# The inverse column transform of a Haar layer: VectorE butterflies in place of matmuls for the first 16 channels of three batches, and the levels of the other chunks placed anew

## The chip, the cores and the metric

The kernel runs on one core of one Trainium2 chip. The metric is the device time of one execution in microseconds (us); of several runs the median is given. The engines of the core work beside each other, each in the order of its own instructions: TensorE (PE, with its weight loads PEld), VectorE (DVE), ScalarE (ACT), GpSimd (POOL), and SyncE (SP), which here issues most of the DMAs.

## What is computed

The input x is (4, 64, 256, 256) in float32: 4 batches of 64 channels. Four layers follow each other. Layers 0, 1 and 3 are a long convolution per channel with a separable filter; layer 2 works on a Haar transform.

```python
# layers 0, 1, 3: the filter of a channel is an outer product of two 256-long filters
k = einsum('ijk,imk->ijmk', hx, hy)
y = irfft2(rfft2(x, s=(512, 512)) * rfft2(k, s=(512, 512)) / 512)[..., :256, :256]
x = y + x * bias[:, None, None]
# layer 2
f1 = haar2d(x)                       # along w, then along h
for i in range(2):
    f4 = einsum('bchw,oc->bohw', f1 * v[i], conv_w[i])     # mixes the 64 channels
    acc += sign(f4) * relu(abs(f4) - tau[i])
x = haar2d(acc, inverse=True) + x
```

One level of the inverse Haar transform takes sums and differences of two halves, a + d and a - d, and doubles the length; eight levels make 256.

## The kernel before, in words

**Convolutions** (`first`, `second`, `contract`, lines 250 to 287). A separable convolution is two products with a Toeplitz matrix, one along each axis. `toeplitz` loads a [128, 2, 256] tile `t` from a padded filter in DRAM by an overlapping access pattern; `contract` makes four float32 matmuls of it (128x256 and 128x128, twice, L253 and L254). The first product goes to PSUM and is copied by ACT (L267), the second is added to the residual by DVE (L284). Layers 0 and 1 give a0, y0, a1, y1 per channel; then `pairs` (L329, L330) takes sums and differences of neighbours, `levels` the further levels along w (DVE L342, L343, then POOL), `store` keeps the result in DRAM, `split`, `rest`, `down` (L361, L366, L373) transform along h by a matmul with the Haar matrix, and `away` (L385, L386) stores the coefficients in DRAM.

**Mixing** (`mixing`, lines 417 to 507). 64 groups per batch. A group loads two rows of coefficients of all channels (f), mixes the channels by 8 matmuls (L441, px), scales (L460 by DVE, L465 by ACT), takes size and sign on ACT (L469, L472), shrinks and signs on DVE (L476, L480), and adds the two terms into z (L486, DVE). z is one tile of SBUF, [128, 4, 128, 4, 16]: 4 chunks of 16 channels each, 128 places along h, 4 x 16 values per place.

**Inverse** (`inverse`, lines 509 to 597). The transform along h is made in one of two ways.
- By butterflies on DVE, in place in z: `level(n, chunk)` calls `halve`, which makes two DVE instructions (L291 a difference, L292 twice the even part less that difference), on 64 n elements each. The levels n = 1, 2, 4, ..., 64 are called for chunks 1, 2 and 3 (channels 16 to 63), n = 32 in two and n = 64 in four pieces of 16 pairs. `butterfly` makes the coarsest step for all chunks.
- For channels 0 to 15 (chunk 0), by a matmul per channel: `halves` splits the row-transformed tile pw into two parts w (ACT L540 and DVE L541), and `cols` multiplies both with the Haar matrix hb (two 128x512 matmuls, L547, pu).

Per channel: `sooner` loads the Toeplitz tile t2, `early` loads r, the untransformed part, from `keep` (tags f with three buffers or f4 with two; f4 holds also w), `fetch` copies the channel out of z (ACT L526, zc), `rows` makes the last steps along w and transposes (6 PE instructions, L533, L534, pw; the pool psx has two buffers), `join` adds r (DVE L555, t, one buffer) and takes sum and difference (L558, L559, u, five buffers). Then the last convolution follows (a3, y3, out), for two of three channels at once; of the third, `aside` stores u in DRAM (late), and its convolution is made during the mixing of the last batch.

**Order.** Work of different stages is interleaved by hand: each stage calls `at(time, run, unit)`, with a tick and a place in it from the table PLACE, and at the end all events run in the order of their times. A tick is one group of mixing or one channel of the inverse. The tile framework then orders each engine's instructions, may move one forward whose inputs are there, and puts in the waits; so the levels 16, 32 and 64 of batches 0 to 2, whose ticks lie in the inverse, stand for the most part in the mixing of the built program. Batch 0's convolutions stand alone at first; those of batch b + 1 are spread over the mixing of batch b, with a tail in the first channels of its inverse. The inverse of batch b runs from tick `start` to `start + 64`, then the mixing of batch b + 1 begins. `along` is the tick at which the batch's mixing starts. The last batch (b + 1 == B) has no convolutions to lay beside its mixing but those put aside, and its chunks' levels stand in its inverse.

Of the kernel before, what the change touches and what calls it, by code (L numbers as in the profile page):

```python
# [12 lines left out]
ALU = mybir.AluOpType  # L13
# [3 lines left out]
B, C, S, EMB, ORD = 4, 64, 256, 33, 64  # L17
# [8 lines left out]
PLACE = {  # L26
    "load": 0.714,
    "a0": 1.643,
    "a0 copy": 1.643,
    "y0": 2.571,  # L30
    "y0 sum": 2.571,
    "a1": 3.5,
    "a1 copy": 3.5,
    "y1": 4.429,
# [64 lines left out]
def conv_seq_kernel(ctx, tc, x, fz, fw, bias, decay, haar, haar_row, factors, vt, taut, wmix, out):  # L99
# [14 lines left out]
    nc = tc.nc  # L114
# [126 lines left out]
    def toeplitz(layer, c, name):  # L241

        t = tp.tile([P, 2, S], F32, name=name, tag="toep")
        nc.sync.dma_start(t, ap(pads[layer], c * 2 * ROW, [[1, P], [ROW, 2], [1, S]]))
        return t
# [40 lines left out]

        return [product, residual]

    def halve(even, odd):

        nc.vector.tensor_sub(odd, even, odd)  # L291
        nc.vector.scalar_tensor_tensor(even, even, 2.0, odd, ALU.mult, ALU.subtract)  # L292

    def level(n, chunk, begin=0, count=None):

        count = n if count is None else count
        v = z.rearrange("p n s x c -> p n s (x c)")[:, chunk].rearrange("p (j e s) x -> p j e s x", e=2, s=P // 2 // n)
        halve(v[:, begin : begin + count, 0, 0, :], v[:, begin : begin + count, 1, 0, :])

    def butterfly():  # L300

        v = z.rearrange("p n s (h k) c -> p n s h k c", k=2)
        for h in range(2):
            halve(v[:, :, 0, h, 0, :], v[:, :, 0, h, 1, :])
# [6 lines left out]
    def at(time, run, unit):  # L311
        events.append((time, len(events), run, unit))
# [196 lines left out]
    def inverse(b, start, put_off):  # L509

        st = {}

        def early(c):
            tag, bufs = ("f", 3) if c < 20 or c % 5 < 3 else ("f4", 2)
            r = mx.tile([P, 2, 2, P], F32, name=f"r_{b}_{c}", tag=tag, bufs=bufs)
            nc.sync.dma_start(r, keep[b][c])
            st[c]["r"] = r

        def sooner(c):
            st[c] = {}  # L520
            if c not in put_off:
                st[c][2] = toeplitz(2, c, f"t2_{b}_{c}")

        def fetch(c):
            a = mx.tile([P, 2, 2, P], F32, name=f"zc_{b}_{c}", tag="mag")
            nc.scalar.copy(a.rearrange("p h k i -> p (h k) i"), z[:, c // 16, :, :, c % 16].rearrange("p i x -> p x i"))  # L526
            st[c]["z"] = a

        def rows(c):
            a = st[c]["z"]  # L530
            ps = psx.tile([P, 2, 2, 2, P], F32, name=f"pw_{b}_{c}", tag="mix")[:, 0]
            for m in range(2):
                nc.tensor.matmul(ps[:, 0, m, :], a[:, 0, m, :], hsinv, start=True, stop=True)  # L533
                nc.tensor.transpose(ps[:, 1, m, :], a[:, 1, m, :], ident)  # L534
            st[c]["pw"] = ps

        def halves(c):
            w = st[c]["w"] = mx.tile([P, 2, 2, 2, P], F32R, name=f"w_{b}_{c}", tag="f4")
            ps = st[c]["pw"]
            nc.scalar.copy(w[:, 0], ps)  # L540
            nc.vector.tensor_tensor(w[:, 1], ps, w[:, 0].bitcast(F32), ALU.subtract)  # L541

        def cols(c):
            ps = psm.tile([P, 2, 2, P], F32, name=f"pu_{b}_{c}", tag="mm")
            flat = "p e m w -> p (e m w)"
            for i in range(2):
                nc.tensor.matmul(  # L547
                    ps.rearrange(flat), hb, st[c]["w"][:, i].rearrange(flat), start=(i == 0), stop=(i == 1)
                )
            st[c]["pw"] = ps  # L550

        def join(c):
            ps = st[c]["pw"]
            t = io.tile([P, 2, 2, P], F32, name=f"t_{b}_{c}", tag="res", bufs=BUFS["res"])
            nc.vector.scalar_tensor_tensor(t, st[c]["r"], 0.5, ps, ALU.mult, ALU.add)  # L555
            u = io.tile([P, 2, S], F32, name=f"u_{b}_{c}", tag="y", bufs=BUFS["y"])
            v = u.rearrange("p m (w e) -> p m w e", e=2)
            nc.vector.tensor_add(v[:, :, :, 0], t[:, 0], t[:, 1])  # L558
            nc.vector.tensor_sub(v[:, :, :, 1], t[:, 0], t[:, 1])  # L559
            st[c]["u"] = u  # L560

        def aside(c):
            nc.scalar.dma_start(late[b, c], st.pop(c)["u"])

        along = start - groups - 3

        def when(tick, n, chunk, *span):
            at(tick + PLACE["level"], lambda _: level(n, chunk, *span), 0)

        at(along + 11 + PLACE["level"], lambda _: butterfly(), 0)  # L570
        for chunk in range(1, 4):
            turn = start + 16 * (chunk - 1)
            for n in (1, 2, 4, 8):
                when(along + 12 + 3 * chunk if b + 1 < B else turn, n, chunk)
            when(turn + 1, 16, chunk)
            for i in range(2):
                when(turn + 2 + 2 * i, 32, chunk, 16 * i, 16)
            for i in range(4):
                when(turn + 6 + 2 * i, 64, chunk, 16 * i, 16)

        for c in range(C):
            for name, stage in zip(("sooner", "early", "fetch", "rows"), (sooner, early, fetch, rows)):
                at(start + c + PLACE[name], stage, c)
            turn = start + c
            if c < 16:
                at(start + c + PLACE["halves"], halves, c)
                at(start + c + PLACE["cols"], cols, c)
                turn += 1
            at(turn + PLACE["join"], join, c)
            if c in put_off:  # L590
                at(turn + PLACE["aside"], aside, c)
            else:
                shift = (0.0, 0.0)
                if put_off:
                    shift = ((-0.27, -0.342), (0.23, 0.158))[c % 3]
                for name, stage in zip(("a3", "a3 copy", "y3", "y3 sum", "out"), last(b, st)):
                    at(turn + PLACE[name] + shift[name[0] != "a"], stage, c)

    def last(b, st):
        return [  # L600
            *first(b, st, "u", 2, "a3"),
            *second(b, st, "a3", 2, "u", "y3", "co"),
            lambda c: nc.scalar.dma_start(out[b, c].rearrange("(k p) w -> p k w", p=P), st.pop(c)["y3"]),
        ]
# [40 lines left out]
    ahead = C  # L645
    start = ready + 3
    for b in range(B):
        mixing(b, start, N_ACT[b])
        end = start + groups + 3
        if b + 1 < B:  # L650
            ready = convolutions(b + 1, spread(ahead, end + 2), in_parts=range(C), border=end)
        else:
            convolution(
                [(i, c) for i in range(B - 1) for c in sorted(put_off)], spread(start - 2, end + 2, (B - 1) * len(put_off))
            )
        inverse(b, end, put_off if b + 1 < B else ())

        start = max(end + C, ready + 3)
        ahead = start - 3
# [114 lines left out]
```

## Time and profile before

| what | value |
|---|---|
| median of 3 runs | 2877.69 us (2876.81 to 2878.61) |
| the profiled execution | 2882.3 us, span of its instructions 2880.5 us |
| granted TensorE clock, mean | 0.998 |
| busy PE / PEld / DVE / ACT / POOL | 2825.3 / 2553.6 / 2504.8 / 2057.4 / 333.1 us |
| DMA | 649.77 MB, mean 226 GB/s |
| batch 0: first mixing matmul, first and last row matmuls | 450.7, 871.4, 1068.2 us |
| batch 1: the same | 1069.6, 1530.5, 1716.8 us |
| batch 2: the same | 1718.2, 2179.0, 2362.4 us |
| batch 3: the same | 2362.5, 2653.1, 2869.6 us |

In the lists of groups each line has the source line, the engine, the operation, out<-in by the names of the tiles, the shapes, the count, then the busy time and the mean time of one, and behind the second bar the idle time of the engine just before these instructions and what ended it. The busy time of an engine is the union of its instructions; an instruction may start before the one in front of it has ended, so a mean duration is more than what the instruction takes from a full engine. A window line gives busy time and count per engine between two times, then the granted clock, the share of the DMA engines and their rate.

### The profile page before, as it was taken

What the parts mean: (1) busy time and instruction counts of PE and PEld (TensorE: products, weight loads), DVE (VectorE), ACT (ScalarE), POOL (GpSimd) and SP (SyncE); (2) the same over time, 40 slices, a digit from 0 to 9 for tenths busy, and PEclk for the clock granted to TensorE, in tenths of its full rate; (3) what the DMA queues carried; (4) which work ended last, traced back from release to release, by engine and by line L of the source; (5) the groups of instructions that cost most, each with busy time, mean ns of one, the idle gap of its engine ahead of it and who ended that gap; (6) DMA issues with size and microseconds to landing.
All of it is one profiled execution on the core that took longest, in us unless ns stands there. A gap on an engine that the chain in (4) does not pass through costs nothing.

```text
span 2880.5 us, 52311 instructions
## 1 busy us (share of the span) xinstructions
PE 2825.3 (98%) x16566; PEld 2553.6 (89%) x16566; DVE 2504.8 (87%) x4263; ACT 2057.4 (71%) x4822; POOL 333.1 (12%) x644
## 2 busy tenths in 40 slices
PE   8999999999999999999999999999999999999999
PEld 6899998888888898998888998998888998888998
DVE  4655558999999779999999779999999779999985
ACT  2333337999995558989995658989995658888554
POOL 0111111121221001121121001121121000000000
PEclk9999999999999999999999999999999999999999
DMA  5877777676666986777777986777777988887786
GB/s 162 247 233 230 232 233 227 204 213 205 201 210 207 285 258 195 215 211 212 214 208 229 302 260 195 215 212 213 213 208 228 300 270 233 237 231 212 224 240 200
DMA packets 599366, 649.77 MB, mean 226 GB/s; under 512 B 48465, under 2 KB 517044, under 8 KB 598964
## 3 DMA queue, kind: packets, MB, share of 16 engines
q1 hardware_dynamic: 519860, 562.09, 67.1%
q10 hardware_dynamic: 79232, 84.34, 8.3%
q8 instruction: 134, 2.20, 0.3%
q14 instruction: 140, 1.15, 0.1%
HBM read 426.77 MB, written 219.48 MB: 224 GB/s over the span
## 4 chain that ended last, share of the span: by engine, by line
PE 47%; DVE 12%; ACT 3%; DMA 3%; issue 2%; POOL 0%; SPq 0%; DVEq 0%; ACTq 0%
PE pa L253 12%; PE py L253 11%; PE px L441 6%; PE pa L254 6%; PE py L254 6%; PE pw L533 4%; DVE mag L480 2%; DVE mag L476 2%; DVE y L284 2%; ACT f L465 2%; PE pw L534 2%; PE pz L373 2%; DVE f L460 1%; DMA t<-pad 1%; DVE z L486 1%
## 5 line engine op out<-in xcount | busy, mean ns | idle before, releaser
L253 PE MATMUL py<-t,a 128*128 128x256 f32 x3072 | 924.1, 383 | 10.1 <-ACT a L267 9.3
L267 ACT COPY a<-pa 128x512 f32<-128x512 f32 x768 | 478.6, 623 | 501.2 <-PE pa L254 462.9
L465 ACT ACTIVATE f<-px,vt 128x64 f32<-128x64 f32 x2688 | 584.7, 367 | 106.1 <-DVE f L460 105.8
L254 PEld LDWEIGHTS py<-t,a 128*128 128x128 f32 x3072 | 584.4, 190 | 79.6
L254 PE MATMUL py<-t,a 128*128 128x128 f32 x3072 | 590.8, 274 | 0.0
L253 PEld LDWEIGHTS py<-t,a 128*128 128x128 f32 x3072 | 497.5, 191 | 52.8 <-ACT a L267 20.1
L441 PE MATMUL px<-wb,f 128*128 128x256 f32 x2048 | 487.2, 380 | 6.3 <-ACT f L465 6.1
L441 PEld LDWEIGHTS px<-wb,f 128*128 128x128 f32 x2048 | 369.2, 190 | 48.0 <-ACT f L465 8.4
L343 POOL TENSOR_TENSOR sd<-less 128x128 f32<-128x128 f32 (+4 forms) x320 | 192.6, 602 | 1869.0 <-DVE less L342 1545.5
L526 ACT COPY zc<-z 128x512 f32<-128x512 f32 x256 | 281.7, 1103 | 107.8 <-PE pw L534 99.5
L476 DVE TENSOR_TENSOR mag<-mag,vt 128x1024 f32<-128x1024 f32 x256 | 312.2, 1220 | 11.5 <-ACT mag L469 10.7
L253 PE MATMUL pa<-t,y 128*128 128x256 f32 x1024 | 309.1, 384 | 7.9 <-DVE y L284 5.2
L480 DVE SCALAR_TENSOR_TENSOR mag<-mag,f 128x1024 f32<-128x1024 f32 x256 | 312.1, 1220 | 0.0
L469 ACT ACTIVATE mag<-f 128x1024 f32<-128x1024 f32 x256 | 295.4, 1154 | 22.9 <-DVE z L486 22.3
L253 PE MATMUL pa<-t,x 128*128 128x256 f32 x1024 | 306.2, 381 | 0.0
L366 DVE TENSOR_TENSOR sp<-sd,sp 128x512 fp32r<-128x512 f32 x256 | 178.7, 698 | 127.5 <-ACT sp L361 126.4
L472 ACT ACTIVATE f<-f 128x1024 f32<-128x1024 f32 x256 | 285.8, 1117 | 3.3
L253 PE MATMUL pa<-t,u 128*128 128x256 f32 x772 | 233.8, 385 | 6.5 <-ACT w L540 2.8
L284 DVE SCALAR_TENSOR_TENSOR y<-x,bsb,py 128x512 f32<-128x512 f32 x256 | 189.5, 740 | 44.6 <-PE py L254 43.6
L254 PEld LDWEIGHTS pa<-t,x 128*128 128x128 f32 x1024 | 194.8, 190 | 26.4
L254 PEld LDWEIGHTS pa<-t,y 128*128 128x128 f32 x1024 | 194.5, 190 | 26.3
L284 DVE SCALAR_TENSOR_TENSOR y<-y,bsb,py 128x512 f32<-128x512 f32 x256 | 189.3, 739 | 29.5 <-PE py L254 29.1
(72 smaller groups left out, 4393.2 us busy)
## 6 DMA issues: line engine op xcount, KB each, us to landing
t<-pad SPq DMA_DIRECT2D x768, 256.0 KB, 4.1
x<-in_x SPq DMA_DIRECT2D x256, 256.0 KB, 3.8
coef<-co SPq DMA_DIRECT2D x256, 256.0 KB, 3.2
f<-coef SPq DMA_DIRECT2D x256, 256.0 KB, 3.2
r<-keep SPq DMA_DIRECT2D x256, 256.0 KB, 4.2
out_y<-y ACTq DMA_DIRECT2D x256, 256.0 KB, 4.3
keep<-sums SPq DMA_DIRECT2D x256, 128.0 KB, 2.9
keep<-sd SPq DMA_DIRECT2D x256, 128.0 KB, 2.9
```

Source lines behind the costliest of these rows:

```text
L253: nc.tensor.matmul(ps[:, m, :], src[:, 0, m * P : (m + 1) * P], t[:, ::-1], start=True, stop=False)
L254: nc.tensor.matmul(ps[:, m, P:], src[:, 1, m * P : (m + 1) * P], t[:, : P - 1 : -1], start=False, stop=True)
L267: nc.scalar.copy(a, s["p" + new])
L284: nc.vector.scalar_tensor_tensor(y, s[res], bsb[:, layer, c : c + 1], s["p" + new], ALU.mult, ALU.add)
L343: engine.tensor_tensor(t[:, :, :, half:length], v[..., 0], v[..., 1], ALU.subtract)
L441: nc.tensor.matmul(ps[:, q, h, :], f[:, q, h * P : (h + 1) * P], wb.rearrange("p r n -> p (r n)"), start=True, stop=True,)
L465: nc.scalar.mul(f4[:, j], px[:, j], scale(g, 0)[:, j : j + 1])
L469: nc.scalar.activation(mag, st[g]["f4"], AF.Abs)
L472: nc.scalar.activation(st[g]["f4"], st[g]["f4"], AF.Sign)
L476: nc.vector.tensor_sub(mag, mag, over(g, 1, 16))
L480: nc.vector.scalar_tensor_tensor(mag, mag, 0.0, st[g]["f4"], ALU.max, ALU.mult)
L526: nc.scalar.copy(a.rearrange("p h k i -> p (h k) i"), z[:, c // 16, :, :, c % 16].rearrange("p i x -> p x i"))
```

## The change

In batches 0, 1 and 2 the matmul way of chunk 0 (`halves`, `cols`) is left out, and `level` is called for all four chunks. The levels n = 1 to 16 of every chunk stand in the mixing; n = 32 of chunks 0 and 1 too, n = 64 of chunk 0 wholly and of chunk 1 by half. The rest (half of n = 64 of chunk 1; n = 32 and 64 of chunks 2 and 3) stands in the inverse, in pieces of 8 pairs (512 elements) instead of 16 (1024), and there the first instruction of a piece is ordered behind the last join that was recorded before it, by a dependence without a semaphore. The joins of channels 0 to 15 come one tick sooner and read pw. As w no longer needs the tag f4, r may use it from channel 4 on instead of 20. The last batch keeps its way and its calls.

```diff
--- before.py
+++ after.py
@@ -286,16 +286,21 @@
 
         return [product, residual]
 
-    def halve(even, odd):
-
-        nc.vector.tensor_sub(odd, even, odd)
+    behind = [None]
+    order = mybir.DependencyInfo(mybir.DependencyClass.NoSync, mybir.DependencyReason.DATA)
+
+    def halve(even, odd, stay=False):
+
+        first = nc.vector.tensor_sub(odd, even, odd)
+        if stay and behind[0] is not None:
+            tc.add_manual_dep(first.ins, behind[0].ins.name, order, reason="not ahead of the joins")
         nc.vector.scalar_tensor_tensor(even, even, 2.0, odd, ALU.mult, ALU.subtract)
 
-    def level(n, chunk, begin=0, count=None):
+    def level(n, chunk, begin=0, count=None, stay=False):
 
         count = n if count is None else count
         v = z.rearrange("p n s x c -> p n s (x c)")[:, chunk].rearrange("p (j e s) x -> p j e s x", e=2, s=P // 2 // n)
-        halve(v[:, begin : begin + count, 0, 0, :], v[:, begin : begin + count, 1, 0, :])
+        halve(v[:, begin : begin + count, 0, 0, :], v[:, begin : begin + count, 1, 0, :], stay)
 
     def butterfly():
 
@@ -511,7 +516,7 @@
         st = {}
 
         def early(c):
-            tag, bufs = ("f", 3) if c < 20 or c % 5 < 3 else ("f4", 2)
+            tag, bufs = ("f", 3) if c < (4 if b + 1 < B else 20) or c % 5 < 3 else ("f4", 2)
             r = mx.tile([P, 2, 2, P], F32, name=f"r_{b}_{c}", tag=tag, bufs=bufs)
             nc.sync.dma_start(r, keep[b][c])
             st[c]["r"] = r
@@ -552,7 +557,7 @@
         def join(c):
             ps = st[c]["pw"]
             t = io.tile([P, 2, 2, P], F32, name=f"t_{b}_{c}", tag="res", bufs=BUFS["res"])
-            nc.vector.scalar_tensor_tensor(t, st[c]["r"], 0.5, ps, ALU.mult, ALU.add)
+            behind[0] = nc.vector.scalar_tensor_tensor(t, st[c]["r"], 0.5, ps, ALU.mult, ALU.add)
             u = io.tile([P, 2, S], F32, name=f"u_{b}_{c}", tag="y", bufs=BUFS["y"])
             v = u.rearrange("p m (w e) -> p m w e", e=2)
             nc.vector.tensor_add(v[:, :, :, 0], t[:, 0], t[:, 1])
@@ -567,22 +572,46 @@
         def when(tick, n, chunk, *span):
             at(tick + PLACE["level"], lambda _: level(n, chunk, *span), 0)
 
+        def piece(tick, n, chunk, begin, count):
+            at(tick + PLACE["level"], lambda _: level(n, chunk, begin, count, stay=tick >= start), 0)
+
         at(along + 11 + PLACE["level"], lambda _: butterfly(), 0)
-        for chunk in range(1, 4):
-            turn = start + 16 * (chunk - 1)
-            for n in (1, 2, 4, 8):
-                when(along + 12 + 3 * chunk if b + 1 < B else turn, n, chunk)
-            when(turn + 1, 16, chunk)
-            for i in range(2):
-                when(turn + 2 + 2 * i, 32, chunk, 16 * i, 16)
+        if b + 1 < B:
+            for chunk in range(4):
+                for n in (1, 2, 4, 8):
+                    when(along + 12 + 3 * chunk, n, chunk)
+                when(along + 20 + 3 * chunk, 16, chunk)
+            for chunk in range(2):
+                for i in range(2):
+                    when(along + 37 + i + 3 * chunk, 32, chunk, 16 * i, 16)
+                for i in range(3 - chunk):
+                    when(along + 43 + 8 * i + 3 * chunk, 64, chunk, 16 * i, 16)
+            when(along + 63, 64, 0, 48, 8)
+            when(start - 0.2, 64, 0, 56, 8)
             for i in range(4):
-                when(turn + 6 + 2 * i, 64, chunk, 16 * i, 16)
+                piece(start + 4 + 2 * i, 64, 1, 32 + 8 * i, 8)
+            for chunk in range(2, 4):
+                turn = start + 20 * chunk - 32
+                for i in range(4):
+                    piece(turn + i, 32, chunk, 8 * i, 8)
+                for i in range(8):
+                    piece(turn + 4 + 2 * i, 64, chunk, 8 * i, 8)
+        else:
+            for chunk in range(1, 4):
+                turn = start + 16 * (chunk - 1)
+                for n in (1, 2, 4, 8):
+                    when(turn, n, chunk)
+                when(turn + 1, 16, chunk)
+                for i in range(2):
+                    when(turn + 2 + 2 * i, 32, chunk, 16 * i, 16)
+                for i in range(4):
+                    when(turn + 6 + 2 * i, 64, chunk, 16 * i, 16)
 
         for c in range(C):
             for name, stage in zip(("sooner", "early", "fetch", "rows"), (sooner, early, fetch, rows)):
                 at(start + c + PLACE[name], stage, c)
             turn = start + c
-            if c < 16:
+            if c < 16 and b + 1 == B:
                 at(start + c + PLACE["halves"], halves, c)
                 at(start + c + PLACE["cols"], cols, c)
                 turn += 1
```

## The prediction

> **What bounds the kernel now.** The page comes first: TensorE (PE) is busy 98% of the span, VectorE (DVE) 87%, ScalarE (ACT) 71%, and half of the chain that ended last is PE. Next I cut the span at the first mixing matmul and the first row matmul of each batch. Batch 1 is clean (batch 2 repeats it). In the windows, the columns after the length are busy us and instructions of PE, PEld, DVE, ACT and POOL, then clock, DMA share and GB/s:
>
> ```profile
> 1069.60:1530.50 460.90, 458.66 (x2582) 413.38 (x2581) 448.93 (x743) 403.44 (x1128) 88.08 (x140) 1.00 0.71 208
> 1530.50:1561.90 31.40, 29.26 (x185) 26.55 (x184) 27.24 (x51) 18.86 (x29) 4.97 (x10) 1.00 0.72 224
> 1561.90:1591.10 29.20, 29.20 (x184) 26.45 (x183) 26.25 (x51) 18.84 (x28) 2.64 (x10) 1.00 0.81 256
> 1591.10:1633.00 41.90, 41.79 (x276) 37.99 (x274) 32.63 (x65) 26.52 (x34) 0.00 (x0) 1.00 0.95 305
> 1633.00:1673.20 40.20, 40.19 (x270) 37.15 (x269) 31.11 (x61) 24.80 (x30) 0.00 (x0) 1.00 0.93 288
> 1673.20:1718.20 45.00, 45.00 (x307) 42.33 (x306) 32.75 (x64) 23.79 (x29) 0.00 (x0) 1.00 0.87 280
> ```
>
> Row 1 is mixing: PE and DVE are both full. The others are the inverse, cut at channels 0, 8, 16, 32, 48: PE is full, DVE idles 4, 3, 9, 9 and 12 us, ACT far more. So PE's work counts in the inverse, and DVE work can be added there up to that idle time; in mixing either engine's work counts.
>
> Batch 0 differs: DVE is as full as PE up to channel 16, and PE idles 5 us in the first eight channels.
>
> ```profile
> 450.70:871.40 420.70, 415.00 (x2301) 370.40 (x2300) 412.77 (x695) 389.28 (x1108) 82.93 (x134) 1.00 0.70 208
> 871.40:905.10 33.70, 28.77 (x174) 25.80 (x172) 31.88 (x49) 17.93 (x26) 3.83 (x8) 0.95 0.59 170
> 905.10:938.90 33.80, 32.68 (x194) 28.20 (x195) 33.59 (x61) 20.02 (x30) 3.76 (x10) 1.00 0.79 245
> ```
>
> Then the prices, from the groups kept apart by shape (mean ns of one before the last bar):
>
> ```profile
> L291 DVE TENSOR_TENSOR z<-z 128x1024 f32<-128x1024 f32 x84 | 101.7, 1216 | 0.1
> L555 DVE SCALAR_TENSOR_TENSOR t<-r,pu 128x512 f32<-128x512 f32 x64 | 43.5, 680 | 4.2 <-PE pu L547 3.8
> L541 DVE TENSOR_TENSOR w<-pw,w 128x512 fp32r<-128x512 f32 x64 | 43.2, 680 | 0.0
> L540 ACT CAST w<-pw 128x512 fp32r<-128x512 f32 x64 | 37.8, 590 | 41.2 <-PE pw L534 28.4 <-DVE y L284 6.2 <-PE pu L547 5.8
> L291 DVE TENSOR_TENSOR z<-z 128x512 f32<-128x512 f32 x12 | 8.0, 681 | 0.0
> ```
>
> These durations overlap the next instruction. The timeline's second column is the duration; what an instruction really takes from a full engine is the distance to the next start:
>
> ```profile
> 1559.84 0.68 DVE L541 TENSOR_TENSOR w<-pw,w 128x512 fp32r<-128x512 f32 x1
> 1560.44 0.67 DVE L555 SCALAR_TENSOR_TENSOR t<-r,pu 128x512 f32<-128x512 f32 x1
> ```
>
> ```profile
> 1244.69 1.22 DVE L291 TENSOR_TENSOR z<-z 128x1024 f32<-128x1024 f32 x1
> 1245.83 0.44 DVE L329 TENSOR_TENSOR sums<-y 128x256 f32<-128x256 f32 x1
> ```
>
> ```profile
> 1561.37 0.71 PE L547 MATMUL pu<-w,hb 128*128 128x512 f32 x2
> 1561.91 0.38 PE L533 MATMUL pw<-hrow,zc 128*128 128x128 f32 x2
> ```
>
> So 512 elements take DVE 0.60 us, 1024 take 1.14; in the same way 256 take 0.34, 128 take 0.20 and 64 take 0.14. The pair of column matmuls takes PE 0.54, one toeplitz contraction 1.30, the six row matmuls of a channel 0.66.
>
> The Trainium skill ("Perfetto Trace Analysis", Identifying the Most-Contended Engine) calls matmul busy time a bad measure and weight-load busy a good one. That is 89% on the page, so by the rule PE has 11% to spare and removing matmuls could bring nothing; by the starts above, which follow each other at 0.54 with no hole, it has almost none, and I go by the starts.
>
> **The change, part by part** (times per batch, batches 0 to 2).
>
> *Removed.* 16 channels x 0.54 = 8.6 us of PE; 16 x 0.59 = 9.4 us of ACT, which idles anyway, counted as nothing; 16 x 0.60 = 9.6 us of DVE.
>
> *Added.* Chunk 0's levels: two instructions at each of 64, 128, 256, 512, 1024, 2x1024 and 4x1024 elements, 2 x (0.14+0.20+0.34+0.60+1.14+2.28+4.56) = 18.5 us of DVE. Thirty pieces (60 instructions) have 512 elements where 30 of 1024 would do: 60 x 0.60 - 30 x 1.14 = 2 us. DVE in all: +11 us per batch.
>
> The skill ("VectorE: DVE Perf Modes", The TRN2 errata) speaks against small pieces: a fixed latency per instruction, fp32 tensor_tensor (N+151)/0.96 ns. By it the split would cost 60 x 0.69 - 30 x 1.22 = 5 us per batch instead of 2, and the total gain would be 8 us less; the durations here agree with the formula (681 and 1216 ns), the distances between starts don't.
>
> *Moved.* The order of the built programs shows where the levels stand. Batch 1: from its first shrink to its first join, 55.8 us of levels before and 42.5 after; behind the first join 0 before (8.4 us of halves there) and 33.6 after. Batch 0: 41.1 before and 42.6 after in front of the first join, 14.7 before and 33.6 after behind it. PE's order is otherwise nearly the same.
>
> I sum that order by the prices above, for the stretches of the windows (PE / DVE work, DVE cut at the joins, us):
> - Batch 1 mixing, to the first row matmul: 455 / 451 before, 455 / 434 after; measured 460.9.
> - Batch 1 channels 0-8, 8-16, 16-32, 32-48: before 29/23, 29/20, 40/29, 39/28; after 29.5/25, 20.5/25, 40/42, 39/36.
> - Batch 0 mixing: 409 / 413 before, 409 / 410 after, but the DVE work of groups 16 to 63 rises from 292 to 301 and PE's there is 290. Channels 0-8, 8-16, 16-32: before 26/32, 31/25, 40/29; after 29/24.5, 21/25, 39/41.5.
>
> *Batches 1 and 2.* Mixing: DVE no longer ties with PE, 2 us of the 6 above PE's sum go (bounds 0 and 6). Channels 0 to 16: PE falls 8.6, but DVE is then the longer one in 8-16 (25 against 20.5), and two row tiles in PSUM let PE run only two channels (about 5 us) ahead, so I book 6 of the 8.6. Channels 16 to 32: DVE 42 against PE 40, costs 2. Net -6 each; bounds 0 and -14.
>
> *Batch 0.* Mixing: DVE has 9 us more in groups 16 to 63 and gives 12 back behind them, too late for PE: +6 (bounds 0, +10). Inverse: before, stretch by stretch, the larger sums make 32+31, measured 67.5; after, 29+25 and the friction of batch 1, 2.4, make 56: -11, and nothing for the dip of the clock to 0.95, which may come again (1.7 us either way). Net -5; bounds +6 and -20.
>
> *Waits that it adds.* Channels 16, 32 and 48 may be fetched (L526, ACT) only after the last piece of their chunk; behind a fetch on ACT stand the copies of a3, and PE waits for those. The last pieces are due 6, 6 and 2 ticks (2.5 us each) ahead, so I book nothing; one late channel costs its delay. The added ordering only places pieces behind a join, it adds no semaphore.
>
> *Queues.* r gets five buffers from channel 4 on, formerly three until 20: SP issues the same loads, some earlier. DVE waited for r 8 times, 8.0 us, in the whole run: 0 (bound -6). Channels 8 to 16 in 25 us instead of 29 would need 256 x 29.2 / 25 = 299 GB/s; the next stretch moved 305, so DMA still covers it. Without that cover, half a microsecond per channel.
>
> Why a DVE this full needn't cost more: in the last batch's inverse (unchanged) levels and halves already stand between the joins, cut at channels 0, 8, 16 and 32:
>
> ```profile
> 2653.10:2679.60 26.50, 26.14 (x166) 23.73 (x167) 26.36 (x43) 17.42 (x24) 0.00 (x0) 1.00 0.61 180
> 2679.60:2709.50 29.90, 29.90 (x194) 27.59 (x193) 29.57 (x50) 17.42 (x24) 0.00 (x0) 1.00 0.69 209
> 2709.50:2764.40 54.90, 54.03 (x356) 49.80 (x356) 54.48 (x90) 25.87 (x31) 0.00 (x0) 1.00 0.80 241
> ```
>
> DVE is 99% busy and PE with it; the fetches there waited 17.3 us for PE and never for a level.
>
> **Sum.** -6 -6 -5 = -17 us. The profiled execution took 2882.3 (span 2880.5, 1.8 around it): 2865.3. The runs' median is 4.6 below that execution: 2860.7, so 2861.
>
> **Rivals.**
> - *PE keeps all it is given.* 3 x 8.6 = 26 us, and batch 0's +6 doesn't come while 4 of its stall go: 2848. For it: DVE's sum from the last shrink to the join of channel 16 falls even in batch 1 (71.5 to 66). Against: DVE is the longer in two stretches of each inverse. 0.20.
> - *Nothing comes of it.* Batch 0's mixing costs 10, each inverse wins 3: 2877.7 + 10 - 9 = 2879. For it: DVE gets 33 us more work in all, on an engine 87% busy. 0.13.
> - *Slower: pieces between a join's first and second instruction.* In the built order most pieces stand there, so u, on which PE's next contraction waits, comes 0.60 to 1.2 us later. If PE waits each time, a batch pays a share of its 33.6 us. Above 8.6 / 33.6 = 26% it loses more than the matmuls gave; at one half, 16.8 - 8.6 = +8 per batch and +6 in batch 0's mixing: 2908. Against: before, PE hardly waits for u (under 2 us in channels 0 to 32), and the last batch stands the same. 0.21.
> - *That it doesn't do what it says*: excluded by the built order (48 column pairs fewer, 33.6 us of levels behind the joins).
>
> **Chances.** Forecast 0.46 (own range 2851 to 2870). About 0.2% of the time, 5.8 us, can be told from no change. Faster: 0.46 + 0.20 = 0.66; same 0.13; slower 0.21. The range leaves out the slower half of the last rival and little below: 2838 to 2890.
>
> **What would show it.** Pairs of pu: 16 left. Right, if batch 1's first row matmul of channel 16 comes about 54 us after channel 0's (60.6 now) and channels 16 to 32 take 43 to 45, with DVE nearly full; if batch 0's mixing is 425 to 428. Wrong, if PE in channels 4 to 32 waits for u or for zc, or if DVE in mixing still ties with PE and the length stays 461.

## The result and the profile after

The changed kernel takes 2885.3 us (median of 8 runs, 2883.7 to 2887.31), the kernel before 2877.66 (8 runs beside them, 2876.64 to 2880.38): a ratio of 1.0024 with the interval [1.0015, 1.0033], 7.6 us **slower**. The forecast was 2861, faster; the time lies inside its range.

The page's first part. TensorE lost 13 us of busy time where the prediction took away 26 us of matmuls, VectorE gained 27 where it added 33; and 32 column matmuls (16 pairs) are left, in a line of the list of groups. Behind the edit, lines have numbers five higher than before (t is L560 now, u L563 and L564, zc L531):

```profile
PE 2812.5 (98%) x16470; PEld 2533.1 (88%) x16470; DVE 2532.3 (88%) x4371; ACT 2034.4 (71%) x4774; POOL 338.4 (12%) x644
...
L552 PE MATMUL pu<-w,hb 128*128 128x512 f32 x32 | 11.9, 443 | 0.3 <-DVE w L546 0.3
```

Batch 1, cut at the same events as before (mixing; inverse from channels 0, 8, 16, 32, 48), columns as in the prediction:

```profile
1069.50:1529.70 460.20, 458.27 (x2582) 413.22 (x2581) 443.20 (x747) 403.82 (x1128) 92.27 (x140) 1.00 0.71 210
1529.70:1561.90 32.20, 30.90 (x198) 28.00 (x197) 24.49 (x47) 16.71 (x23) 2.86 (x10) 1.00 0.82 245
1561.90:1588.60 26.70, 23.43 (x142) 19.84 (x141) 25.98 (x52) 13.01 (x16) 4.18 (x10) 1.00 0.72 222
1588.60:1631.60 43.00, 42.21 (x274) 37.90 (x272) 40.72 (x79) 27.57 (x37) 0.00 (x0) 1.00 0.89 278
1631.60:1674.10 42.50, 40.99 (x271) 37.07 (x270) 40.68 (x80) 24.01 (x30) 0.00 (x0) 1.00 0.90 289
1674.10:1719.80 45.70, 45.46 (x307) 42.16 (x306) 32.87 (x65) 23.22 (x29) 0.00 (x0) 1.00 0.87 274
```

Before, TensorE was full from channel 8 on and VectorE had room. Now in channels 8 to 16 VectorE is busy 25.98 of 26.7 us and TensorE only 23.43; in 32 to 48 it is 40.68 of 42.5, and that stretch is 2.3 us longer than before. The work has moved to the other engine, and that engine is now the full one.

Batch 0, its mixing and channels 0 to 8 and 8 to 16:

```profile
447.00:880.60 433.60, 418.61 (x2300) 370.81 (x2299) 421.90 (x709) 390.01 (x1108) 82.54 (x136) 1.00 0.69 203
880.60:912.30 31.70, 30.40 (x196) 27.61 (x194) 23.26 (x44) 15.69 (x21) 0.86 (x5) 1.00 0.79 241
912.30:940.00 27.70, 23.63 (x144) 20.11 (x143) 26.66 (x53) 14.01 (x18) 4.18 (x10) 1.00 0.75 223
```

The mixing takes 12.9 us more (420.7 before; 1.7 of it is a dip of the clock, see the last section), the inverse 9.3 less (198.2 before, 188.9 now).

The whole balance in the profiled executions: start -3.7 us (it scatters between 446.4 and 450.9 over all runs), batch 0 +3.6, batch 1 +1.7, batch 2 +1.5, batch 3 0: +3.1, and the spans differ by 3.0. The medians differ by 7.6 because the profiled execution of before lay 4.6 us above its median.

What the new bound does to TensorE is seen in the timeline of channels 8 to 16 (start, duration, engine, line; the wait in brackets):

```profile
1569.95 0.68 DVE L560 SCALAR_TENSOR_TENSOR t<-r,pw 128x512 f32<-128x512 f32 x1
...
1570.54 0.69 DVE L297 SCALAR_TENSOR_TENSOR z<-z 128x512 f32<-128x512 f32 x1
...
1571.15 0.42 DVE L563 TENSOR_TENSOR u<-t 128x256 f32<-128x256 f32 x1
...
1571.48 0.42 DVE L564 TENSOR_TENSOR u<-t 128x256 f32<-128x256 f32 x1
...
1571.82 1.29 DVE L294 TENSOR_TENSOR z<-z 128x512 f32<-128x512 f32 x2
...
1571.96 0.70 PE L253 MATMUL pa<-t,u 128*128 128x256 f32 x2 [0.28 <-DVE u L564]
```

VectorE starts one instruction right behind the other. A butterfly piece (L297) stands between t and u, so u starts 1.20 us behind t (right behind each other it is 0.72, see the last section), and the last convolution on TensorE waits for u.

### The profile page after: what moved, and what is told of

Read it like the earlier page. It is cut to its first block, busy times and chain, and to the rows that moved or that the text cites. A ratio compares the mean times of both kernels' runs of the same rounds, so it can differ in the third digit from the quotient of the medians.

```text
span 2883.5 us, 52198 instructions
## 1 busy us (share of the span) xinstructions
PE 2812.5 (98%) x16470; PEld 2533.1 (88%) x16470; DVE 2532.3 (88%) x4371; ACT 2034.4 (71%) x4774; POOL 338.4 (12%) x644
## 5 line engine op out<-in xcount | busy, mean ns | idle before, releaser
L253 PEld LDWEIGHTS py<-t,a 128*128 128x128 f32 x3072 | 495.2, 191 | 56.3 <-ACT a L267 25.5
L531 ACT COPY zc<-z 128x512 f32<-128x512 f32 x256 | 279.3, 1106 | 113.9 <-PE pw L539 96.7
L481 DVE TENSOR_TENSOR mag<-mag,vt 128x1024 f32<-128x1024 f32 x256 | 318.2, 1243 | 12.0 <-ACT mag L474 11.5
L485 DVE SCALAR_TENSOR_TENSOR mag<-mag,f 128x1024 f32<-128x1024 f32 x256 | 318.4, 1245 | 0.0
L284 DVE SCALAR_TENSOR_TENSOR y<-y,bsb,py 128x512 f32<-128x512 f32 x256 | 190.4, 744 | 30.3 <-PE py L254 30.1
```

The source lines that it names most:

```text
L253: nc.tensor.matmul(ps[:, m, :], src[:, 0, m * P : (m + 1) * P], t[:, ::-1], start=True, stop=False)
L284: nc.vector.scalar_tensor_tensor(y, s[res], bsb[:, layer, c : c + 1], s["p" + new], ALU.mult, ALU.add)
L481: nc.vector.tensor_sub(mag, mag, over(g, 1, 16))
L485: nc.vector.scalar_tensor_tensor(mag, mag, 0.0, st[g]["f4"], ALU.max, ALU.mult)
```

## The experiments

Two theories stood at first. **Amount** (A in the texts): VectorE now has more work than TensorE in some stretches, wherever the pieces stand in them. **Place** (B): the pieces stand in front of the join's instructions that TensorE waits for. The stage times of all runs, from their traces (us; batch 1 is cut at channels 0, 8, 16, 32, 48):

| run | median | ratio [95%] | b0 mixing | b0 inverse | b1 mixing | 0-8 | 8-16 | 16-32 | 32-48 | 48- |
|---|---|---|---|---|---|---|---|---|---|---|
| before | 2877.66 | 1 | 420.7 | 198.2 | 460.9 | 31.4 | 29.1 | 42.0 | 40.2 | 45.0 |
| after | 2885.3 | 1.0024 [1.0015, 1.0033] | 433.6 | 188.9 | 460.2 | 32.1 | 26.7 | 43.0 | 42.5 | 45.7 |
| only0 | 2883.63 | 1.0015 [1.0006, 1.0024] | 433.5 | 188.9 | 461.1 | 31.4 | 29.2 | 41.7 | 40.2 | 45.0 |
| only12 | 2882.61 | 1.0011 [1.0002, 1.0020] | 421.7 | 197.8 | 460.3 | 32.1 | 26.7 | 44.2 | 42.5 | 45.4 |
| alone | 2892.1 | 1.0043 [1.0029, 1.0057] | 424.8 | 198.5 | 460.5 | 41.0 | 23.4 | 40.7 | 41.2 | 45.0 |
| held | 2892.29 | 1.0046 [1.0034, 1.0059] | 421.4 | 196.6 | 458.4 | 35.4 | 30.3 | 44.2 | 42.5 | 45.2 |
| no_c0 | 2871.48 | 0.9971 [0.9960, 0.9981] | 421.4 | 188.9 | 458.4 | 32.1 | 26.7 | 43.8 | 42.5 | 45.2 |
| no64 | 2872.72 | 0.9978 [0.9969, 0.9989] | 432.0 | 184.9 | 460.3 | 32.1 | 25.5 | 41.1 | 41.1 | 45.0 |
| behind_u | 2890.31 | 1.0039 [1.0024, 1.0054] | 433.7 | 191.1 | 460.3 | 32.1 | 26.6 | 43.8 | 43.3 | 45.4 |
| inplace | 2884.95 | 1.0019 [1.0010, 1.0029] | 432.0 | 179.3 | 470.8 | 30.0 | 26.0 | 42.8 | 42.0 | 36.9 |
| wide | 2902.4 | 1.0075 [1.0059, 1.0090] | 432.0 | 197.3 | 460.2 | 34.3 | 27.4 | 44.3 | 42.9 | 45.3 |
| spread | 2873.68 | 0.9979 [0.9969, 0.9989] | 431.9 | 185.2 | 460.3 | 32.5 | 23.2 | 43.5 | 41.5 | 45.1 |
| gap | 2872.35 | 0.9973 [0.9963, 0.9982] | 421.2 | 198.9 | 460.9 | 32.1 | 24.3 | 43.0 | 39.8 | 45.1 |
| gap012 | 2879.0 | 1.0002 [0.9993, 1.0011] | 442.0 | 184.0 | 460.7 | 32.1 | 24.3 | 43.0 | 39.8 | 45.2 |
| mixed | 2872.1 | 0.9979 [0.9970, 0.9988] | 432.9 | 185.5 | 460.7 | 32.1 | 24.3 | 43.0 | 39.8 | 45.1 |
| fine0 | 2875.93 | 0.9990 [0.9981, 0.9999] | 437.0 | 185.8 | 460.7 | 32.1 | 24.3 | 43.0 | 39.8 | 45.1 |

Each ratio is against the kernel before on the same chip. A stage that two runs share mostly comes out within 0.5 us, but for dips of the clock (1.7 us each, 3.4 for the long ones of `wide`, `inplace` and `fine0`), so stage times tell apart what medians don't. Single stretches differ by more without a dip (channels 16 to 32 take 44.2 in `only12` and 43.0 in after), so one of about 1 us in one batch proves little.

**Where: one batch or the others.** In `only0` the change is made in batch 0 alone, in `only12` in batches 1 and 2 alone.

```diff
-        if b + 1 < B:
+        if b in NEW:          # only0: (0,)   only12: (1, 2)
... the same for the buffers of r and for halves and cols
```

> The change in batch 0 alone, batches 1 and 2 as before. Theory A (VectorE is the longer engine where levels were put: in groups 16 to 63 of batch 0's mixing, and in channels 8 to 48 of every inverse): batch 0 lost 11 us in its mixing and won 6 in its inverse, so 5 us over before, 2883. Rival B (not the amount of VectorE work but its place: pieces between the instructions of a join, in every inverse alike): a third of the loss, 2.5 us, 2880. Rival C (TensorE's clock dips or DMA, nothing of the levels): 2878.

> The change in batches 1 and 2 alone, batch 0 as before. Theory A: 1 to 2 us over before in each of the two, 2880 to 2881. Rival B: two thirds of the loss, 5 us, 2883. Rival C: 2878.

Both lose, by 0.15% and 0.11%; these totals alone don't tell A from B, but their stages are those of before and after, put together. So there are two losses, of different kinds: batch 0 pays in its mixing, batches 1 and 2 in their inverse.

**Which half of the change: alone and held.** `alone` takes the matmuls out and puts all of chunk 0's levels into the mixing, the other chunks' calls as before. `held` keeps the matmuls and has only the new calls.

```diff
 alone:  for chunks 1 to 3, in place of the pieces
+                for i in range(2):
+                    when(turn + 2 + 2 * i, 32, chunk, 16 * i, 16)
+                for i in range(4):
+                    when(turn + 6 + 2 * i, 64, chunk, 16 * i, 16)
...
 held:
-            for chunk in range(4):
+            for chunk in range(1, 4):
...
-            if c < 16 and b + 1 == B:
+            if c < 16:
```

> Chunk 0 wholly by butterflies in batches 0 to 2, but the levels of chunks 1 to 3 at their old ticks and with no ordering behind the joins, so that the built program puts them in front of channel 8 again. Theory A: in channels 0 to 8 VectorE has 40 us of work beside 29 of TensorE, which eats what the missing matmuls give; 0 to 2 us over before in each batch, 2880 to 2884. Rival B: no piece stands behind a join, so the 26 us of the matmuls show, 2855 to 2862.

> The placement alone: chunk 0 by the matmuls as before, the levels of chunks 1 to 3 placed as in the change (pieces of 8 pairs behind the joins). Theory A: batch 0's mixing is freed of VectorE's excess (5 us less), but in batches 1 and 2 VectorE becomes the longer engine in channels 8 to 32 while TensorE keeps its matmuls: 7 us more each; about 2886. Rival B: the pieces cost what they cost in the change and the matmuls come on top, 26 us over the change, 2911.

Neither half by itself is faster than before or than the whole, and both came out slower than theory A had them (2880 to 2884 and 2886). A part of `alone`'s 12 us is dips of the clock: its executions had a mean clock of 0.996 to 0.998, those of before on that chip 0.999 to 1.000, and with all dips taken out its profiled batches are 4.4, 1.5 and 1.0 us over before. In `alone` nothing is held back, and yet batch 1's first eight channels take 41.0 us, with VectorE full and TensorE not:

```profile
1071.10:1531.60 460.50, 458.56 (x2583) 413.07 (x2582) 449.89 (x753) 403.94 (x1128) 96.84 (x140) 1.00 0.71 210
1531.60:1572.60 41.00, 33.09 (x198) 29.23 (x197) 40.07 (x65) 16.89 (x23) 7.45 (x13) 0.96 0.65 201
```

VectorE's 449.89 us in the mixing are what it had before (448.93): it was already full there, so as much work as is added comes out behind. That refutes place as the only cause and speaks for amount. `held` gives the prices of the halves, read from batch 2, which has no dip of the clock: the pieces in the inverse cost 9.2 us (183.5 to 192.7), the mixing gains 2.4, and the matmuls, when they go too, give 7.1 (192.7 to 185.6). In `held`'s mixing VectorE has 20 us less than before:

```profile
1064.80:1523.30 458.50, 457.57 (x2583) 413.25 (x2583) 428.54 (x724) 405.03 (x1128) 84.54 (x140) 1.00 0.72 210
```

TensorE is busy 457.57 of 458.5 us. That is near the floor of the stage: 20 us of relief to VectorE bought 2.4 there and cost 9.2 in the inverse. In the whole change chunk 0's levels fill the mixing again and take back 1.7 of the 2.4 (458.5 to 460.2); so 9.2 - 7.1 - 0.7 makes batch 2's loss of about 1.5.

**Batch 0's mixing: no_c0.** In batches 0 to 2 all calls of `level` for chunk 0 are left out (so its channels aren't transformed along h, but for the coarsest step); that is 18.5 us of VectorE per batch by the prediction's prices.

```diff
-            for chunk in range(4):
+            for chunk in range(1, 4):
...
-            for chunk in range(2):
+            for chunk in range(1, 2):
...
-            when(along + 63, 64, 0, 48, 8)
-            when(start - 0.2, 64, 0, 56, 8)
```

> The change, with chunk 0's levels left out in batches 0 to 2 (the output is wrong by that; 18 us of VectorE per batch in the mixing). Theory A: batch 0's mixing gives back its 11 us, those of batches 1 and 2, where TensorE is the longer one, at most 2 each; the inverses stay: 2885 less 12 to 15, 2870 to 2873. Rival E (what batch 0's mixing lost comes from where the pieces of level 64 stand or from the dip of the clock there, not from the amount): chunk 1's pieces stay, so at most half, 2879 to 2883.

Batch 0's mixing goes from 433.6 (431.9 without its dip) back to 421.4. The same 310 us of it, 546 to 856, in before, after and this run:

```profile
546.00:856.00 310.00, 306.25 (x1696) 273.77 (x1696) 305.67 (x498) 293.87 (x842) 65.00 (x100) 1.00 0.69 208
```

```profile
546.00:856.00 310.00, 297.54 (x1627) 263.09 (x1626) 302.65 (x490) 281.75 (x807) 64.77 (x98) 0.99 0.67 198
```

```profile
546.00:856.00 310.00, 305.51 (x1694) 273.01 (x1693) 301.50 (x493) 293.53 (x842) 60.51 (x100) 1.00 0.69 207
```

In after, VectorE is as busy as ever (302.65), but TensorE gets 69 matmuls fewer done (1627 against 1696). The waits in that window say through what: first before, then after (engine, line, waited for: us, times, longest):

```profile
ACT f L465 <- DVE f L460: 9.8, 17, 2.0
```

```profile
ACT f L470 <- DVE f L465: 14.2, 9, 3.4
PEld px L446 <- ACT f L470: 11.1, 10, 2.3
```

ScalarE scales behind VectorE's scaling, and now the mixing matmuls wait for ScalarE, up to 2.3 us at a time.

**The crowd in the inverse: no64.** The 64-butterfly levels of chunks 2 and 3 are left out in batches 0 to 2 (the result lacks them).

> The change, with the level n = 64 of chunks 2 and 3 left out in batches 0 to 2 (16 pieces, 19 us of VectorE per batch behind the joins; the output is wrong by that). Theory A (VectorE is the longer engine in channels 8 to 48 of each inverse): each inverse falls back to what TensorE needs, 7 to 9 us less, 24 in all: 2861. Rival D (TensorE's own order, the two row tiles, ACT or the DMAs set the pace there, and VectorE is only busy beside it): at most 5 us in all, 2880.

Between the two: some 13 us less than after by the ratios (0.9978 against 1.0024), more than rival D's 5, but not 24. Channels 32 to 48 gain 1.4 of the 2.3 us by which they had grown, as 7.8 us of VectorE's busy time left them; and channels 8 to 12 take what they take in after, 13.83 us with VectorE busy 13.64 and TensorE 12.12: there the rest of chunk 1 and the 32-butterflies of chunk 2 (one per channel from channel 8) fall together. So VectorE's work does set the pace, and it seems to count where pieces meet and not in the sum over an inverse. How long such a stretch is, and whether it is the lead that two row tiles in PSUM allow TensorE, is an argument, not a measurement.

**Order within a channel: behind_u.** Pieces are ordered behind the join's last instruction instead of its first.

```diff
-            behind[0] = nc.vector.scalar_tensor_tensor(t, ...)
+            behind[0] = nc.vector.tensor_sub(v[:, :, :, 1], t[:, 0], t[:, 1])
```

> The change, but each held piece is ordered behind the last of a join's three instructions instead of the first. Rival B (it is the place between t and u that delays TensorE's next contraction): u comes 0.6 us sooner where a piece stood, 2 to 6 us per batch less, 2867 to 2879. Theory A: the same VectorE work, and fewer pieces to fill the gaps between the three dependent instructions: 0 to 2 us more per batch, 2885 to 2891.

No gain (1.0039 against 1.0024; the intervals overlap), so the place within the channel isn't it. TensorE's waits in batch 1's inverse hardly change: 2.9 us for u and 3.1 for t, against 2.7 and 2.8 in after.

**inplace.** The join writes over r instead of the one buffer of t.

```diff
-            t = io.tile([P, 2, 2, P], F32, name=f"t_{b}_{c}", tag="res", ...)
-            nc.vector.scalar_tensor_tensor(t, st[c]["r"], 0.5, ps, ...)
+            t = st[c]["r"]
+            nc.vector.scalar_tensor_tensor(t, t, 0.5, ps, ...)
```

> The change, but the join writes its first result over r instead of into t, which has one buffer. In the trace of the change t follows u after 0.51 us and not 0.34, since t's buffer must be read out first. Theory A with this price (0.17 us in about half of 40 channels where VectorE is the longer engine): 2 to 4 us per batch less, 2874 to 2880. If VectorE isn't the longer one there, or that wait is hidden: 2885.

Inconclusive. The tile framework then laid 64 matmuls of the next batch's first convolutions behind the inverse (712 convolution matmuls in batch 1's inverse, 776 in after): that inverse is 177.7, but the mixing 470.8, and channels 8 to 48 gain only 1.4. One thing shows: right behind u the join's first instruction now starts after 0.34 to 0.35 us instead of 0.51, so the 0.51 was the price of t's one buffer.

**Length of a piece: wide.** Pieces of 16 pairs (1024 elements), half as many, in the same stretches.

```diff
-                for i in range(8):
-                    piece(turn + 4 + 2 * i, 64, chunk, 8 * i, 8)
+                for i in range(4):
+                    piece(turn + 5 + 4 * i, 64, chunk, 16 * i, 16)
```

> The change with held pieces of 16 pairs (1024 elements) instead of 8, the same ticks on average. By the distances between starts the split costs 60 ns per instruction, about 2 us per batch of VectorE work; where it is the longer engine 1 to 2 us per batch come back, 2879 to 2882. By a fixed latency as in the durations, 4 to 5 us per batch: 2872. If a piece of 1.14 us between t and u holds TensorE up more than two of 0.60: 2888.

The slowest run, 0.5% over after (five times the 3 us that the third case had), though VectorE has hardly more or less to do (50.60 us busy in channels 0 to 16 of batch 1, 50.47 in after): every stretch up to channel 48 is longer. TensorE's own waits in channels 0 to 16 of batch 1, first in after, then in this run:

```profile
PE pa L253 <- DVE u L564: 2.0, 5, 0.7
PE pw L538 <- DVE t L560: 1.9, 2, 1.0
```

```profile
PE pw L538 <- DVE t L560: 3.5, 4, 1.3
...
PE pa L253 <- DVE u L564: 2.4, 4, 0.8
```

It waits 2 us more for the joins, and the stretch is 2.9 us longer. So, as the third case of the expectation had it, the length of the one piece that stands in front of a join counts as well as the amount. But a piece of twice the length is also two short ones at one place, so this run doesn't tell length from spacing.

The Trainium skill ("VectorE: DVE Perf Modes", The TRN2 errata) advises tiles of 512 elements or more, as a large one pays the fixed latency once; both lengths here meet that. By its formula `wide` should have won some 13 us (an estimate: 56 instructions of 512 elements against 28 of 1024, 4.4 per batch). The runs show the opposite sign, and what they show with it are TensorE's longer waits for the joins behind the pieces.

**The cure: spread.** The same 28 pieces, one every 1.5 channels.

```diff
+            held = [(64, 1, 32 + 8 * i) for i in range(4)]
+            for chunk in range(2, 4):
+                held += [(32, chunk, 8 * i) for i in range(4)] + [(64, chunk, 8 * i) for i in range(8)]
+            for i, (n, chunk, begin) in enumerate(held):
+                piece(start + 4 + 1.5 * i, n, chunk, begin, 8)
```

> The change with the same 28 pieces behind the joins, one every 1.5 channels from channel 4 on, in place of two rows of pieces that fall together in channels 8 to 11 and 28 to 31. Theory A narrowed (VectorE is the longer engine for stretches of three or four channels, since TensorE can run only two row tiles ahead; sums over eight channels hide it): channels 8 to 16 go from 26.7 to about 24 us, the rest stays, 2 to 3 us per batch less, 2876 to 2880. If only the sum over the inverse counts: 2885.

2873.68, 0.9979 [0.9969, 0.9989] of before, with the same instructions as after; the gain over after, about 4 us per batch, is more than was expected. The stretches from channels 0, 8, 16 and 32 of batch 1:

```profile
1525.30:1557.80 32.50, 30.89 (x198) 28.02 (x196) 24.86 (x49) 16.64 (x23) 3.27 (x11) 1.00 0.82 242
1557.80:1581.00 23.20, 22.33 (x142) 19.74 (x142) 23.13 (x46) 11.76 (x16) 3.33 (x9) 1.00 0.81 259
1581.00:1624.50 43.50, 42.51 (x275) 37.80 (x273) 43.09 (x85) 27.79 (x38) 0.00 (x0) 1.00 0.89 284
1624.50:1666.00 41.50, 41.38 (x269) 37.21 (x270) 40.82 (x81) 24.57 (x30) 0.00 (x0) 1.00 0.88 278
```

Channels 8 to 16 take 23.2 instead of 26.7; TensorE's busy time there is 22.33 where it was 23.43, the rest of the difference is its idle time. That spacing alone gives 4.3 us in batch 1's inverse and 3.7 in batch 0's shows that where the pieces stand, and not their sum over the inverse, made the inverse longer than before. It doesn't show that sums over eight channels hide the crowd, as its expectation had it: channels 8 to 16 have 11 butterfly instructions here and 16 in after, so their sum fell too. In channels 32 to 48 it does come down to spacing: 19 such instructions against 18, and yet 41.5 us against 42.5, TensorE idle for 0.1 us instead of 1.5.

**gap, gap012, mixed.** `gap` leaves batch 0 as before and, in the next two, fills the mixing up to what VectorE had there before; the 20 pieces left come every second channel. `gap012` does so in batch 0 too; `mixed` takes `spread` for batch 0.

```diff
...
+            for i, tick in enumerate((along + 57, along + 61, along + 64.5, start - 0.1)):
+                when(tick, 64, 1, 32 + 8 * i, 8)
+            for i in range(4):
+                when(start - 3 + i, 32, 2, 8 * i, 8)
+            held = [(64, 2, 8 * i) for i in range(8)] + [(32, 3, 8 * i) for i in range(4)] + [(64, 3, 8 * i) for i in range(8)]
+            for i, (n, chunk, begin) in enumerate(held):
+                piece(start + 4 + 2 * i, n, chunk, begin, 8)
```

> Batch 0 as before; in batches 1 and 2 the change with the rest of chunk 1 and level 32 of chunk 2 moved from the inverse to the end of the mixing, where VectorE has 11 us less work than TensorE, and the 20 pieces left held one every two channels. Theory A: the mixing stays at 460 to 461 us, the inverse comes to 183 to 186 (187.6 before, 190 in the change), so 2869 to 2875 in all. If the pieces delay the mixing by what they cost (9.6 us each batch): 2890.

> What it does: the placement of run gap (the rest of the second chunk and the 32-butterfly levels of the third at the end of the mixing, one piece every two channels) in the first batch as well as in the next two. Both theories that are left are about local stretches. If only VectorE's crowding in three or four channels counts, the first batch's inverse, 199 us in gap, becomes about 183 to 185, its mixing, 421 us, becomes about 432 because the first chunk's levels ride in groups 16 to 63 (as in all runs that put them there), and the whole is some 4 us below gap: 2867 to 2870 us. If the pieces moved into the first batch's mixing lengthen it once more, by the 10 us that the first chunk's pieces cost there, the first batch gains nothing and the whole is 2873 to 2879 us.

> What it does: the first batch takes the even spacing of run spread (28 pieces, one every 1.5 channels), the next two the placement of run gap. If the stages add, which all runs so far bear out, the first batch takes 617 us (mixing 432, inverse 185), the next two 645 and 641, and the whole is 3 us below gap, 2869 us (2867 to 2871). If a gain in one stage is given back in the next, it is 2873 or more.

`gap`, 2872.35, as expected, has the lowest ratio of the kernels that leave nothing out, 0.9973 [0.9963, 0.9982]; the intervals of `spread` and `mixed` overlap with it. Its mixing is 460.9 as before, with VectorE at 449.5, and its inverse 184.3 (187.6 before). `gap012` is 0.3% slower than `gap`: eight pieces more in batch 0's mixing cost about 7 us of it (442.0, of which two dips make 3.4, against 431 to 432 without dips), most of it behind group 63 (32.1, 1.7 of it a dip, instead of 24.1), as its expectation had it for its second case. `mixed` equals `gap` within the intervals, and the 3 us that were expected of it don't show: without the dips, one in `mixed` and two in `gap`, batch 0 takes 616.7 us in both.

**Amount or length in batch 0's mixing: fine0.** As `mixed`, with the levels 16 to 64 in batch 0's mixing in pieces of 8 pairs.

> What it does: run mixed, and in the first batch's mixing the levels 16, 32 and 64 of the chunks are called in pieces of 8 pairs (512 elements) instead of 16, at about the same groups; the work is the same but for 1 us of VectorE. If the first batch's mixing is 432 us instead of 421 because VectorE's amount of work there (301 us in groups 16 to 63) is more than TensorE's 290, it stays at 431 to 434 and the whole is within 1 us of mixed. If it is the length of one piece, which holds up the scaling f that ScalarE and then the mixing matmuls wait for (14 us of such waits in the changed kernel, 9 before), the mixing falls to 422 to 427 and the whole lies 5 to 10 us below mixed, at 2859 to 2864 us, and ScalarE's wait for f at 9 to 11 us.

Its mixing is 437.0; less one dip of the clock of 6.83 us at 769 us (3.4 lost) it is 433.6, no better than `mixed` (432.9, with a dip that loses 1.7). ScalarE's wait for f is 13.2, and the median is 3.8 us over `mixed`. So shorter pieces don't bring the 5 to 10 us that the length as the cause would have meant, and by `no_c0` the amount is. The length is not cleared altogether: group 48 begins 305.4 us into this mixing, 6.4 sooner than in `spread` (311.8, without a dip), and the lead is lost in one stall near 765 us, with the dip behind it, in which VectorE waits 3.4 us for ScalarE and ScalarE 3.0 for GpSimd.

## Why the prediction was wrong

Its sum was -6 -6 -5; measured in the profiled stages it is +1.7, +1.5 and +3.6 (about +5 without the clock dips: two in batch 0 before, one after). The two largest misses are channels 0 to 16, with 4.3 us in each of two batches, and batch 0's mixing, with 5 to 7.

- **What bounds the kernel**: half right. In the inverse VectorE's work is free only up to its idle time, as it said (though TensorE was not full in channels 0 to 8: 29.26 of 31.4). In the mixing of batches 1 and 2 the engines don't count alike: TensorE is the bound, and VectorE has no room for more, but taking from it brings little.
- **Mixing of batches 1 and 2, -2 (0 to -6)**: -0.7. VectorE's busy time in the window fell only 5.7 us, where its sums had 17, and `held` shows that even 20 us are worth 2.4, as TensorE is full at 457.57.
- **Channels 0 to 16, "6 of the 8.6"**: this step failed first. Measured -1.7 (60.5 to 58.8). The prediction's own sums allowed less than it booked: 29 + 29 before, 29.5 + 25 after is -3.5, not -6. In channels 8 to 16 VectorE sets the time (busy 25.98 of 26.7 us), most of all in 8 to 12, where pieces of two chunks meet (13.64 of 13.83), and TensorE's lead of two row tiles didn't carry it over: TensorE idles 3.3 us there. With the pieces spaced (`spread`) it is -4.8. The sign of being wrong that it named came: in channels 0 to 16 TensorE waits for u five times.
- **Channels 16 to 32, +2**: +1.0. **Channels 32 to 48, nothing booked**: +2.3. There the sum of starts, 36 of VectorE against 39 of TensorE, was too low: VectorE is busy 40.68 of 42.5. By the same prices the instructions that start between the row matmuls of channels 32 and 48 make 38.8 (and 39.0, not 42, in 16 to 32). The price 0.60 for t holds only with another instruction between; u right behind t starts 0.72 later, and t right behind u mostly 0.51 later instead of 0.34. These pairs stand 6 and 5 times there, and y, 11 times, takes 0.66: 6 x 0.12 + 5 x 0.17 + 11 x 0.06 = 2.2 us more.
- **Batch 0's mixing, +6 (0 to +10)**: +11 without the dip. The 9 us of VectorE work added in groups 16 to 63 come whole and 2 more; +6 had counted on a part being hidden. `no_c0` gives 10.5 of it back, shorter pieces (`fine0`) bring nothing.
- **Batch 0's inverse, -11**: -9.3, of which before's two dips are 3.4. What the change does is -6; channels 8 to 16 crowd as in the other batches (27.7).
- **Queues, fetches**: right. TensorE waited for zc 1.6 us in the whole run (3.3 before), and the DMAs moved at most 289 GB/s in a stretch of batch 1.

Of the rivals, "slower" has the direction; its figure, 2908, is further off than that of "nothing comes of it", 2879. It said that the pieces lose more than the matmuls gave once 26% of their time shows; `held` shows 9.2 / 33.6 = 27%. With 27% its sum would be 2885, which would be luck, since batch 0 lost in its mixing and not in its inverse. Its mechanism, pieces between t and u, is half right: `wide` shows that long pieces cost more, `behind_u` that moving them away from that place gains nothing, `spread` that their distance from each other counts. Its price for batch 0 (+6) was too low too.

The evidence from the last batch, where a full VectorE and a full TensorE stood beside each other, misled: full engines say nothing of what one more piece costs. The 8 us that it gave for the skill's formula are 9 by its own figures, 3 x (5 - 2).

Open: of the 8.6 us of matmuls per inverse the best run keeps 3.3. Channels 16 to 32 give 1.0 of it back (43.0 against 42.0), and channels 0 to 8 of batch 1, 31.4 before, take 32.1 or more in all runs without the matmuls but `inplace`. The trace shows why: 24 convolution matmuls more start there than before (144 against 120) and 12 column matmuls fewer, by the prediction's prices 3 x 1.30 - 6 x 0.54 = +0.7 us; channels 8 to 16 have as many convolution matmuls fewer, and VectorE is full there. What t's one buffer costs in all is not settled, as `inplace` changed the order too.

## What to carry over

Where two engines are both nearly full, moving work from one to the other is not judged by the stage's sum: look for the short stretches in which the moved pieces meet (how short was not measured). If the moved work can be spaced, space it evenly and in small pieces; the same instructions were 0.4% faster so. And fill first the stage where the other engine is the bound by itself, up to what it bore before (`gap`, 0.7 to 0.8 us per batch shorter than `spread`), and no further (`gap012`, 7 us in batch 0's mixing).

## What was not expected of the hardware

- VectorE's distance between starts depends on what follows: t to u 0.72 us right behind each other, 0.60 with a piece or y between; u to t 0.51 with t's one buffer against 0.34 to 0.35 in `inplace`; y, with the bias as a third operand, 0.66 for the same 512 elements.
- The granted clock is halved for 3.41 us at a time (now and then 6.83), costing 1.7 us, up to four times (in `alone`) in a profiled execution, whose mean clock is 0.998 to 1.000 all the same. It comes again at the same places in kernels that share the schedule there: near 885 and 943 us in before, `only12` and `gap` (batch 0 as before), near 597 in after and `only0`; `no_c0`, `no64` and `spread` have none before the last microseconds.
- It follows TensorE's waits. Before each of the 24 dips in all traces (the last microseconds left out) lie 3.41 us in which TensorE was busy for 0.9 to 1.6 us, its longest pause 0.9 to 2.5 us; of some 13,000 other stretches of that length, cut in step with the dips, only 3 were no busier than the busiest of these. The dip of after and the stretch in front of it:

```profile
593.40:596.80 3.40, 1.51 (x8) 1.00 (x7) 3.40 (x5) 3.40 (x13) 0.00 (x0) 1.00 0.34 105
596.80:600.20 3.40, 3.40 (x12) 2.86 (x11) 1.75 (x2) 3.23 (x5) 0.00 (x0) 0.50 0.46 154
```

So by the traces a dip is not chance that falls on a run but a further price of the waits before it, and stage times "without the dips" leave that price out. No run was made to test this.
